# A hybrid Mamba/attention network on one core: the skip term D u on VectorE, and a PSUM bank of its own for each head's scores

## The chip, the cores and the metric

The kernel runs on one core of a Trainium2 chip. Five engines work from queues of their own, each in order: TensorE (PE; its weight loads are shown as PEld), VectorE (DVE), ScalarE (ACT), GpSimd (POOL) and SyncE (SP), which issues nearly all DMA transfers here. They meet through semaphores. Matmul results go to PSUM, which has eight banks of 512 fp32 columns in 128 partitions. The metric is the device time of one execution in microseconds.

## The reference

The input is x of (8, 384, 32, 32) in fp32: eight images (batches) of 1024 tokens with 384 channels. Two layers follow each other.

Layer 0 normalizes the tokens and runs a selective scan over them forward and, with the same weights, backward. For one direction (u is the convolved input after SiLU, z the gate, 16 states n per channel):

```python
def step(h, inp):
    dA, dBu, c = inp
    h = dA * h + dBu
    return (h, jnp.einsum('bdn,bn->bd', h, c))
...
y = ys.transpose(1, 0, 2) + u * D_param
y = y * silu(z)
return jnp.einsum('bld,od->blo', y, out_proj_w)
```

The two directions are added, scaled, joined with a local 3x3 convolution branch, and added to x.

Layer 1 is causal self-attention with 6 heads of 64, and then, on batches in 5 groups of one (`8 // 5`), a feed-forward network of width 1536 with sign-binarized weights and a quantization by the maximum of each group:

```python
scores = jnp.einsum('bhqd,bhkd->bhqk', q, k)
scores = jnp.where(causal, scores, -jnp.inf)
attn = jax.nn.softmax(scores, axis=-1)
out = jnp.einsum('bhqk,bhkd->bhqd', attn, v)
```

Batches past the fifth get attention only, since the groups don't reach them.

## The kernel before

Everything is fp32, with channels on the 128 partitions (3 chunks c of 384) and tokens along the free axis, in halves h of 512. A fp32 matmul shows as two MATMUL records.

**Stages.** For each batch there is `before_scan` (norm, input projections, convolutions, gates, delta), then the scan in units, then `attention`, and for five batches `feed_forward`. The program emits these as lists of small steps with rough costs. `spread_over` and the due times at the end of the function interleave them: scan units of later batches run beside attention, feed-forward and the `before_scan` of others. The last batch's attention stands alone at the end. The Tile framework then lays out each engine's queue by priorities and ready times of its own model, and gives tiles their buffers: a tile with a tag waits until one of the tag's `bufs` buffers is free.

**Scan.** A unit is one batch, one chunk c, one direction and half (`part`), and two states n: 768 units in all. `s_first` (L588) multiplies on GpSimd into a tile g (six buffers). `s_scan` makes exp(delta A) on ScalarE (L601), runs two scans on VectorE (L606) and one more GpSimd product (L612). `s_sum` (L620) adds the two states up over units: eight TensorE transposes of g into the PSUM bank y. After the last transposes g is free again. L636 and L641 take y to SBUF (yt).

**Gate.** `s_gate` runs 48 times, once for each batch, chunk and half. It loads halves of us (the sum of both directions' u) and of silu(z), each into a tile with one buffer (the DMA issues are recorded at L112, in `load`). In a bank of tag "pt" a matmul with the diagonal matrix diagd (L656) puts D u, and the transposes of the one or two yt tiles are added on it (L661). VectorE multiplies with the gate (L670), and SP stores the result (L672).

**Attention.** Heads go in pairs, two heads e to a chunk c: head e has partitions 64e to 64e+63 of q and k. `probabilities` calls `scores` 288 times in all: two matmuls (L788) into two PSUM tiles `ss`, one for each head, with e=1 first; the second, e=0, has a raised priority and is pinned behind what TensorE had before it in the program. Then, e=0 first, VectorE's tensor_tensor_reduce (L802, which shows as a custom instruction and a read of the accumulator) adds the mask, moves the tile out to SBUF and makes the row's extreme nm, and ScalarE takes the exponential (L812). `weighted_values` turns the probabilities over (L864, L866) and multiplies them with v (L877).

**PSUM banks.** `bank` hands out tiles of one bank each under five tags: y 1, da 2, s 2, pt 2, av 1, so all eight banks are taken. A call without a tag alternates between s and pt. Tag "s" serves the scores, the feed-forward matmuls (hp, yp, yq), and every other one of the projections (op, qp, vp, ap) and norms.

`pin` is the framework's `keep_in_program_order`: an instruction may not be queued ahead of the one that the program has before it on the same engine. It sets the order only, not a wait for its end, and others may come between.

Of the kernel before, what the change touches and what calls it, by code (L numbers as in the profile page):

```python
# [12 lines left out]
ALU = mybir.AluOpType  # L13
# [4 lines left out]
P = 128  # L18
B, C, H, W = 8, 384, 32, 32
L = H * W  # L20
NC = C // P
# [28 lines left out]
V_NORM, V_CW, V_CB, V_DTB, V_D, V_DW, V_DWB, V_BP, V_B2, V_ALOG = 0, 1, 5, 6, 7, 8, 17, 18, 19, 20  # L50
# [4 lines left out]
def kernel(  # L55
# [16 lines left out]
    nc = tc.nc  # L72
    pin = tc.keep_in_program_order
# [10 lines left out]
    def ctile(name, shape, dt=F32):  # L84
        return const.tile(shape, dt, name=name, tag=name)
# [4 lines left out]
    def mtile(name, n=L):  # L90
        return mid.tile([P, n], F32, name=name, tag="mid")
# [1 line left out]

    BANKS = {"y": 1, "da": 2, "s": 2, "pt": 2, "av": 1}
    turn = [0]

    def bank(name, tag=None):
        if tag is None:  # L100
            turn[0] += 1
            tag = ("s", "pt")[turn[0] % 2]
        return ps.tile([P, HB], F32, name=name, tag=tag, bufs=BANKS[tag])

    def half(h):
        return slice(h * HB, (h + 1) * HB)

    def chunk(c):
        return slice(c * P, (c + 1) * P)

    def load(dst, src):
        nc.sync.dma_start(out=dst, in_=src)  # L112
# [17 lines left out]
    vec = ctile("vec", [P, NC, NV])  # L130
# [8 lines left out]
    for d in range(2):  # L139
        nc.scalar.dma_start(out=wdt[d * DW : d * DW + RANK, :], in_=w_dt)  # L140
        nc.scalar.dma_start(
            out=wdt[d * DW + RANK : d * DW + RANK + 1, :],
# [13 lines left out]
    ident = ctile("ident", [P, P])  # L156
# [21 lines left out]
    amat = ctile("amat", [P, NC, NS])  # L178
    nc.scalar.activation(amat, vec[:, :, V_ALOG : V_ALOG + NS], AF.Exp)
    nc.vector.tensor_scalar(amat, amat, -1.0, None, ALU.mult)  # L180
    diagd = ctile("diagd", [P, NC, P])
    for c in range(NC):
        nc.vector.tensor_scalar(diagd[:, c, :], ident, vec[:, c, V_D : V_D + 1], None, ALU.mult)
    rssm = ctile("rssm", [P, 1])
    nc.vector.tensor_tensor(rssm, sc[:, 0:1], sc[:, 1:2], ALU.mult)
    rsh = ctile("rsh", [P, 1])
# [9 lines left out]
    def binarize(src, dst, nk, nout, per, name, emit):  # L196
# [15 lines left out]
        @emit  # L212
        def _():
            st["mps"] = bank(f"mps_{name}", "av")
# [44 lines left out]
    def mean_of(c_of, name):  # L259

        m = bank(name)
        for c in range(NC):
            nc.tensor.matmul(out=m, lhsT=onesc, rhs=c_of(c), start=(c == 0), stop=(c == NC - 1))  # L263
        return m
# [42 lines left out]
    def before_scan(b, tags, emit, later=None, diags=None):  # L307
# [5 lines left out]
        def bank_of(name):  # L313
            return bank(name, next(turns))
# [328 lines left out]
    def s_gate(u):  # L643

        if not u.last:
            return
        b, c, h = u.b, u.c, u.h
        yts = sst.pop(("yt", b, c, h))
        both = []
        for what in ("us", "z"):  # L650
            t = sp.tile([P, HB], F32, name=f"{what}h_{u.name}", tag=what, bufs=1)
            load(t, spilled[b, what, c][:, half(h)])
            both.append(t)
        us, sz = both
        tp = bank(f"yb_{u.name}", "pt")
        nc.tensor.matmul(  # L656
            out=tp, lhsT=diagd[:, c, :], rhs=us, start=True, stop=False, skip_group_check=True
        )
        for yt in yts:
            for i in range(QT):  # L660
                nc.tensor.matmul(  # L661
                    out=tp[:, chunk(i)],
                    lhsT=yt[:, i, :],
                    rhs=ident,
                    is_transpose=True,
                    start=False,
                    stop=(yt is yts[-1] and i == QT - 1),
                    skip_group_check=True,
                )
        nc.vector.tensor_tensor(sz, sz, tp, ALU.mult)  # L670
        t = dram.tile([P, HB], F32, name=f"sgy_{u.name}", tag=f"sp_gy_{c}_{h}")
        nc.sync.dma_start(out=t, in_=sz)  # L672
        spilled[b, "gy", c, h] = t


    def attention(b, emit_ffn, emit):
# [83 lines left out]
        def at_once(second):  # L760
            return tc.high_priority(offset=HURRY) if second else nullcontext()

        def rows_of(e):
            return slice(e * HD, (e + 1) * HD)

        def blocks_of(n):
            return [(k0, min(k0 + HB, n)) for k0 in range(0, n, HB)]

        def probabilities(c, g, steps):


            nb = g + 1

            def scores(i, qi, n, kb, k0, k1):
                pr = mtile(f"pr_{b}_{c}_{qi}_{kb}").rearrange("p (e l) -> p e l", e=2)
                st["pr", c, g, i, kb] = pr
                if kb == 0 and i == 0:
                    for what in ("nm", "rs"):
                        st[what, c, g] = small.tile(
                            [P, QT, 2, nb], F32, name=f"{what}_{b}_{c}_{g}", tag=f"{what}{nb}"  # L780
                        )
                nm, rs = st["nm", c, g], st["rs", c, g]
                ss = [bank(f"s_{b}_{c}_{qi}_{kb}_{e}", "s") for e in range(2)]

                order = (1, 0)
                for e in order:
                    with at_once(e == order[1]):
                        mm = nc.tensor.matmul(  # L788
                            out=ss[e][:, : k1 - k0],
                            lhsT=st["q"][rows_of(e), c, chunk(qi)],  # L790
                            rhs=st["k"][rows_of(e), c, k0:k1],
                            start=True,
                            stop=True,
                        )
                    if e == order[1]:
                        pin(mm)

                w = k1 - k0
                mask = cmask[:, HB - w :] if k1 == n else cmask[:, :1].to_broadcast([P, w])
                for e in range(2):  # L800
                    x, m = pr[:, e, :w], nm[:, i, e, kb : kb + 1]
                    nc.vector.tensor_tensor_reduce(  # L802
                        out=x,
                        in0=ss[e][:, :w],
                        in1=mask,
                        scale=-1.0,
                        scalar=-MASKED,
                        op0=ALU.add,
                        op1=ALU.min,
                        accum_out=m,  # L810
                    )
                    nc.scalar.activation(  # L812
                        x, x, AF.Exp, bias=m, scale=-1.0, accum_out=rs[:, i, e, kb : kb + 1]
                    )

            for i in range(QT):
                qi = g * QT + i
                n = (qi + 1) * P
                for kb, (k0, k1) in enumerate(blocks_of(n)):
                    steps(lambda i=i, qi=qi, n=n, kb=kb, k0=k0, k1=k1: scores(i, qi, n, kb, k0, k1))  # L820
# [275 lines left out]
    def slots(lo, hi):  # L1096
        def at(f, k):
            if 0 <= k < len(units):
                f(units[k])

        def slot(k):
            at(s_load, k + AHEAD + 2)
            at(lambda u: s_row(u, 0), k + AHEAD + 2)
            at(lambda u: s_row(u, 1), k + 2)
            at(s_first, k + AHEAD)
            at(s_scan, k)
            at(s_sum, k - 1)
            at(s_gate, k - 2)

        return [(lambda k=k: slot(k), 5.0) for k in range(lo, hi)]  # L1110
# [113 lines left out]
```

## Time and profile before

| what | value |
|---|---|
| median of 3 runs | 4989.93 us |
| lowest, highest | 4987.43, 4991.37 us |
| profiled execution | 4984.05 us |
| its span, first to last instruction | 4982.3 us |
| mean granted TensorE clock | 0.884 |
| scores, TensorE (L788) | 1152 records, 384.5 us occupied |
| scores, VectorE (L802) | 576 instructions, 299.5 us, 545 ns mean |
| gate, D u matmul (L656) | 96 records, 60.0 us occupied |
| gate, product (L670) | 48 instructions, 32.0 us |
| scans, VectorE (L606) | 1536 instructions, 1859.8 us |

Busy time is the time in which an engine had at least one instruction under way, so two matmuls side by side count once. A row of the profile's groups gives line, engine, operation, output and inputs, shapes and count, then the busy time with the mean of one instruction in ns, and after the second bar the idle time of the engine just before, with what ended it. A row of the waits gives engine and line, what was waited for, the sum in us, the number of times and the longest.

The attention stage runs from about 928 us for the first batch; the last batch's fills the end from about 4770 us on, with its scores from 4847 us.

### The profile page before, as it was taken

How to read it: one execution, taken by the hardware profiler on the slowest of the kernel's cores; microseconds unless marked ns; L12 is line 12 of the kernel's file. 1: busy time of each engine (PE TensorE's matmuls, PEld its weight loads, DVE VectorE, ACT ScalarE, POOL GpSimd, SP SyncE). 2: the span in 40 equal slices, each digit the busy share in tenths (PEclk: the TensorE clock that was granted, in tenths of full speed). 3: DMA queues.
4: the chain of work that ended last, by engine and by line, in shares of the span. 5: the costliest groups of instructions: out<-in, count | busy, mean ns of one | idle time of the engine just before them, and what ended most of it. 6: DMA issues, size and time to landing. Idle time of an engine off the chain costs nothing. (4 is left out here: it accounts for less than half of the span.)

```text
span 4982.3 us, 50788 instructions
## 1 busy us (share of the span) xinstructions
PE 4058.8 (81%) x16458; PEld 2192.3 (44%) x16458; DVE 3607.8 (72%) x4771; ACT 2668.1 (54%) x4858; POOL 3696.0 (74%) x1944
## 2 busy tenths in 40 slices
PE   3687786988888888788787888887888988888989
PEld 1243343544444444345443444443454544444444
DVE  6887988677886768786778867687867676676623
ACT  4575655565554655545656446555456365464425
POOL 0578687997768986779876788867789888888800
PEclk7788797899989899888998888998899988999999
DMA  6554646324463335463334633334533333334210
GB/s 230 204 185 151 200 164 229 114 93 130 140 220 120 112 116 168 136 200 123 100 125 147 210 111 129 112 130 157 193 130 116 113 110 124 131 102 137 93 58 26
DMA packets 365010, 696.36 MB, mean 140 GB/s; under 512 B 30104, under 2 KB 88904, under 8 KB 364744
## 3 DMA queue, kind: packets, MB, share of 16 engines
q1 hardware_dynamic: 355232, 676.97, 40.9%
q10 hardware_dynamic: 9512, 16.15, 0.9%
q8 instruction: 130, 2.13, 0.2%
q14 instruction: 136, 1.11, 0.1%
HBM read 527.33 MB, written 165.68 MB: 139 GB/s over the span
## 5 line engine op out<-in xcount | busy, mean ns | idle before, releaser
L588 POOL TENSOR_TENSOR g<-ud,bc 128x1024 f32<-128x1024 f32 x768 | 1840.4, 2396 | 579.8 <-PE y L620 452.0
L612 POOL TENSOR_TENSOR g<-g,bc 128x1024 f32<-128x1024 f32 x768 | 1822.1, 2373 | 251.7 <-DVE g L606 157.8
L601 ACT ACTIVATE da<-dl,amat 128x512 f32<-128x512 f32 x1536 | 1057.3, 691 | 1532.5 <-DVE g L606 1498.3
L606 DVE TENSOR_TENSOR_SCAN g<-da,g 128x512 f32<-128x512 f32 x768 | 906.5, 1210 | 475.4 <-POOL g L588 457.2
L606 DVE TENSOR_TENSOR_SCAN g<-da,carry,g 128x512 f32<-128x512 f32 x768 | 953.3, 1271 | 384.2 <-POOL g L588 354.1
L620 PE MATMUL y<-ident,g 128*128 128x128 f32 x6144 | 949.1, 303 | 266.7 <-POOL g L612 123.1
L620 PEld LDWEIGHTS y<-ident,g 128*128 128x128 f32 x6144 | 789.3, 156 | 714.4 <-issue 418.9
L788 PE MATMUL s<-k,q 64*128 64x512 f32 (+3 forms) x1152 | 384.5, 600 | 128.9 <-DVE nm L802 110.5
L802 DVE CUSTOM_DVE_ANT_0 pr<-s,cmask 128x512 f32<-128x512 f32 (+3 forms) x576 | 299.5, 545 | 178.2 <-PE s L788 177.9
L812 ACT ACTIVATE pr<-pr,nm 128x512 f32<-128x512 f32 (+3 forms) x576 | 348.9, 607 | 123.5 <-DVE nm L802 121.6
L864 PE MATMUL pt<-ident,pr 128*128 128x128 f32 x1728 | 304.0, 309 | 93.6 <-ACT ptn L866 55.1
L995 PE MATMUL hp<-t,w 128*128 128x512 f32 x720 | 334.9, 610 | 28.7 <-DMA w<-w1s 18.3
L1039 PE MATMUL yp<-h,w 128*128 128x512 f32 x720 | 332.6, 620 | 15.3 <-DMA w<-w2s 12.1
L864 PEld LDWEIGHTS pt<-ident,pr 128*128 128x128 f32 x1728 | 217.7, 155 | 245.0 <-ACT ptn L866 110.3
L877 PE MATMUL av<-ptn,v 128*64 128x512 f32 (+3 forms) x1152 | 273.1, 555 | 50.4 <-ACT ptn L866 33.9
L341 PE MATMUL in<-xn,win 128*128 128x512 f32 x576 | 282.3, 636 | 32.3 <-DVE xc L463 8.6
L866 ACT COPY ptn<-pt 128x512 f32<-128x512 f32 (+3 forms) x576 | 255.3, 472 | 49.8 <-PE pt L864 48.4
L727 PE MATMUL qp<-t,wqk 128*128 128x512 f32 x576 | 266.4, 613 | 11.7 <-DVE t L302 9.1
L400 DVE SCALAR_TENSOR_TENSOR loc<-xn,vec,loc 128x496 f32<-128x496 f32 (+3 forms) x384 | 259.9, 721 | 19.5 <-ACT loc L389 18.2
L788 PEld LDWEIGHTS s<-k,q 64*128 64x128 f32 x1152 | 132.3, 206 | 261.2 <-DVE nm L802 179.6
L611 POOL COPY carry<-g 128x2 f32<-128x2 f32 x384 | 87.0, 226 | 205.9 <-DVE g L606 205.8
L1039 PEld LDWEIGHTS yp<-h,w 128*128 128x128 f32 x720 | 142.0, 201 | 189.1 <-issue 169.4
(153 smaller groups left out, 4722.4 us busy)
## 6 DMA issues: line engine op xcount, KB each, us to landing
bc<-rows SPq DMA_DIRECT2D x512, 512.0 KB, 4.1
dl<-sdl SPq DMA_DIRECT2D x160, 256.0 KB, 2.9
ud<-sud SPq DMA_DIRECT2D x160, 256.0 KB, 2.7
t<-st SPq DMA_DIRECT2D x63, 512.0 KB, 5.1
su<-u SPq DMA_DIRECT2D x48, 512.0 KB, 3.4
du<-su SPq DMA_DIRECT2D x96, 256.0 KB, 3.8
sdl<-du SPq DMA_DIRECT2D x96, 256.0 KB, 2.8
sud<-du SPq DMA_DIRECT2D x96, 256.0 KB, 2.3
```

Source lines behind the costliest of these rows:

```text
L341: nc.tensor.matmul(out=mp, lhsT=st["win", c][:, k, i, :], rhs=st["xn"][:, k, half(h)], start=(k == 0), stop=(k == NC - 1),)
L588: pin(nc.gpsimd.tensor_tensor(g, ud, sst["bc", 0, u.b, u.part, u.n], ALU.mult))
L601: nc.scalar.activation(da, sst["dl", u.b, u.c, u.part], AF.Exp, scale=amat[:, u.c, n : n + 1])
L606: nc.vector.tensor_tensor_scan(gi[:, ::step], da[:, ::step], gi[:, ::step], first, ALU.mult, ALU.add)
L612: pin(nc.gpsimd.tensor_tensor(g, g, sst["bc", 1, u.b, u.part, u.n], ALU.mult))
L620: nc.tensor.matmul(out=y[:, j, :], lhsT=g[:, i, chunk(j)], rhs=ident, is_transpose=True, start=(u.opens and i == 0 and j == 0), stop=(u.cl ...
L788: mm = nc.tensor.matmul(out=ss[e][:, : k1 - k0], lhsT=st["q"][rows_of(e), c, chunk(qi)], rhs=st["k"][rows_of(e), c, k0:k1], start=True, st ...
L802: nc.vector.tensor_tensor_reduce(out=x, in0=ss[e][:, :w], in1=mask, scale=-1.0, scalar=-MASKED, op0=ALU.add, op1=ALU.min, accum_out=m,)
L812: nc.scalar.activation(x, x, AF.Exp, bias=m, scale=-1.0, accum_out=rs[:, i, e, kb : kb + 1])
L864: nc.tensor.transpose(pt[:, chunk(i)], pr[:, e, chunk(j % QT)], ident)
L995: nc.tensor.matmul(out=hp, lhsT=st["w1"][:, c, chunk(m % 2)], rhs=st["xn"][:, c, half(h)], start=(c == 0), stop=(c == NC - 1),)
L1039: nc.tensor.matmul(out=yp, lhsT=st["w2", k // 6][:, k % 6, :], rhs=st["h", k // NC][:, k % NC, half(h)], start=(k == 0), stop=(k == NF - 1),)
```

## The change

Two edits that don't depend on each other.

In the gate the matmul with diagd is gone, and with it diagd itself. The first transpose now starts the bank, and after the last one VectorE adds us times D to the bank, in PSUM, ahead of the product with silu(z).

The tag "s" with two buffers becomes two tags with one buffer each, s0 and s1. Callers that ask for "s" get them in turn, by a counter of their own, in program order. `scores` asks for s0 for e=0 and for s1 for e=1. The VectorE instruction that empties the bank of e=1 (`order[0]`, the head whose matmul goes first) is pinned behind the one of e=0.

```diff
-    BANKS = {"y": 1, "da": 2, "s": 2, "pt": 2, "av": 1}
-    turn = [0]
+    BANKS = {"y": 1, "da": 2, "s0": 1, "s1": 1, "pt": 2, "av": 1}
+    turn = [0, 0]
...
             tag = ("s", "pt")[turn[0] % 2]
+        if tag == "s":
+            turn[1] += 1
+            tag = ("s0", "s1")[turn[1] % 2]
         return ps.tile([P, HB], F32, name=name, tag=tag, bufs=BANKS[tag])
...
-    diagd = ctile("diagd", [P, NC, P])
-    for c in range(NC):
-        nc.vector.tensor_scalar(diagd[:, c, :], ident, vec[:, c, V_D : V_D + 1], None, ALU.mult)
...
         tp = bank(f"yb_{u.name}", "pt")
-        nc.tensor.matmul(
-            out=tp, lhsT=diagd[:, c, :], rhs=us, start=True, stop=False, skip_group_check=True
-        )
         for yt in yts:
             for i in range(QT):
                 nc.tensor.matmul(
...
-                    start=False,
+                    start=(yt is yts[0] and i == 0),
                     stop=(yt is yts[-1] and i == QT - 1),
                     skip_group_check=True,
                 )
+        nc.vector.scalar_tensor_tensor(tp, us, vec[:, c, V_D : V_D + 1], tp, ALU.mult, ALU.add)
         nc.vector.tensor_tensor(sz, sz, tp, ALU.mult)
...
-                ss = [bank(f"s_{b}_{c}_{qi}_{kb}_{e}", "s") for e in range(2)]
+                ss = [bank(f"s_{b}_{c}_{qi}_{kb}_{e}", f"s{e}") for e in range(2)]
...
-                    nc.vector.tensor_tensor_reduce(
+                    moved = nc.vector.tensor_tensor_reduce(
...
+
+                    if e == order[0]:
+                        pin(moved)
```

## The prediction

> **What bounds the kernel now.** I read the page from the top. Its first part gives the engines' shares, its second shows that no engine is full for the whole run:
>
> ```profile
> PE 4058.8 (81%) x16458; PEld 2192.3 (44%) x16458; DVE 3607.8 (72%) x4771; ACT 2668.1 (54%) x4858; POOL 3696.0 (74%) x1944
> ...
> PE   3687786988888888788787888887888988888989
> DVE  6887988677886768786778867687867676676623
> POOL 0578687997768986779876788867789888888800
> PEclk7788797899989899888998888998899988999999
> ```
>
> TensorE is the busiest engine, at 8 to 9 tenths nearly everywhere. GpSimd, which makes two passes over every scan unit, fills 7 to 9 tenths between slice 2 and slice 38. VectorE passes 8 tenths only in some slices. PEclk says that TensorE ran at 0.7 to 0.9 of its clock, and the page's mean is 0.884.
>
> Next I asked who waits for whom, and for the stages with scores the busy time by window:
>
> ```profile
> POOL g L588 <- PE y L620: 452.0, 202, 14.1
> PE s L788 <- DVE nm L802: 110.5, 89, 3.4
> SPq L112 <- PE yb L656: 201.5, 34, 22.4
> SPq L112 <- DMA sgy<-zh: 51.0, 32, 4.7
> ...
> 928.00:1150.00 222.00, 178.77 (x1005) 103.41 (x1004) 162.79 (x270) 141.21 (x325) 205.79 (x109) 0.91 0.30 98
> 2270.00:2470.00 200.00, 157.85 (x881) 91.89 (x881) 146.35 (x254) 123.26 (x287) 181.45 (x94) 0.89 0.37 119
> 4840.00:4982.00 142.00, 132.37 (x705) 64.62 (x703) 53.67 (x183) 82.50 (x232) 0.00 (x0) 0.98 0.06 23
> ```
>
> The columns of the windows are the stretch, its length, and the busy time of PE, PEld, DVE, ACT and POOL. In the two attention stages shown POOL is 93% and 91% busy, PE 81% and 79%. Over all seven attention stages beside scans (1662 us) POOL is busy for 1473 us, so 189 us are idle, and 174 us of that is POOL waiting for the transposes of L620, which free its buffers g and stand late in TensorE's queue. So TensorE paces POOL there through its order. In the last stage (from 4840 us) there is no scan left and PE is 93% busy: work taken off it there comes off the end directly.
>
> **The scores' matmuls.** The groups by form show what the change aims at, beside the gate's rows:
>
> ```profile
> L788 PE MATMUL s<-k,q 64*128 64x512 f32 x576 | 221.5, 716 | 39.7 <-DVE nm L802 39.4
> L877 PE MATMUL av<-ptn,v 128*64 128x512 f32 x576 | 165.9, 656 | 16.5 <-DVE o L891 16.5
> L656 PE MATMUL yb<-ush,diagd 128*128 128x512 f32 x96 | 60.0, 712 | 3.7 <-ACT ptn L866 1.8 <-DVE du L527 1.1 <-ACT u L379 0.5
> L369 DVE SCALAR_TENSOR_TENSOR u<-up,vec,u 128x512 f32<-128x512 f32 x90 | 66.0, 745 | 3.4 <-ACT u L358 3.3
> ...
> 2283.70 2.07 PE L788 MATMUL s<-k,q 64*128 64x512 f32 x2
> 2285.70 0.90 PE L620 MATMUL y<-ident,g 128*128 128x128 f32 x3
> 2286.53 2.07 PE L788 MATMUL s<-k,q 64*128 64x512 f32 x2
> ...
> 2289.36 2.10 PE L788 MATMUL s<-k,q 64*128 64x512 f32 x4
> ```
>
> One fp32 matmul is two records. A pair of heads uses the array's upper and lower 64 rows. At 2289.36 all four records of a pair took 2.10 us side by side (at a low clock); at 2283.70 and 2286.53 each head's two records took 2.07 us alone, 4.14 us for the pair. In the last stage a full-clock pair takes 1.13 us side by side. L877 has the same columns and counts, all side by side: 165.9 us of occupancy against 221.5.
>
> **What the Trainium skill says.** "TensorE: Matmul & The Clock Gate", section "The mechanism" (of packing small matmuls): matmuls in different row groups run together, so a pack costs about one matmul. The trace agrees (2.10 us against 2 x 2.07). "TensorEngine Tiling (Array Packing)", section "Gotcha 1: PSUM Pressure": row tiles write to different banks and may not share one at a time. So a pair needs both banks free, and the 110.5 us above are that wait. The same first page, section "What's actually happening": a TensorE that was idle runs at half clock until it has been busy for a while. The doubled durations at 2283 us fit; so relief of TensorE may come back in part as a lower clock.
>
> **The change part by part, against the profiled execution** (4984.05 us, span 4982.3; the median of the runs shown is 5.9 us above it).
>
> 1. *Own banks and the tied order.* Before, the head that goes first (e=1) takes whichever of two banks is free, and the other waits for VectorE: half-array runs. After, e=1 needs s1, whose reader is tied behind that of s0, so both are free when e=1 starts, and e=0 follows at once. Occupancy: L788 now takes 221.5+77.7+49.6+36.0 = 384.8 us over its four widths, L877 165.9+47.5+36.1+23.6 = 273.1. In the last stage a paired L788 takes 0.05 us more than a paired L877 (1.13 to 1.08, 0.92 to 0.87), so 273.1 + 288 x 0.05 = 287.5 us is to be had: 97 us less. Not all of it is time: the first matmul ran in a gap that now is waiting, unless something else is queued there. Following the 288 pairs through the trace, 148 aren't in step (or ran at a low clock); if each starts only when both banks are empty and nothing fills the wait, they end some 37 us earlier in sum. Bounds 37 and 97; I take 60, since the order of TensorE's queue is laid out with the wait known, and other ready work (L620, L864) can go ahead.
>
> 2. *D u leaves TensorE.* 96 records, 60.0 us (1.25 us per gate, 48 gates), go. Their weight loads lie beside other work. diagd's three instructions at 15 us (0.8 us) go too and VectorE has 12 us of waiting for DMA there: 0.
>
> 3. *D u comes to VectorE.* 48 scalar_tensor_tensor of 128x512, one operand and the result in PSUM. Nearest row L369, same kind: 66.0/90 = 0.73 us each, 35 us in sum. "VectorE: DVE Perf Modes", "The perf-mode tier table", gives fp32 with a PSUM operand one element per cycle, which agrees. Behind it on VectorE stand the gate's L670 and then scans. The gate itself gets shorter: 1.25 + 1.16 (eight transposes, 55.5/48) + 0.67 before, 1.16 + 0.73 + 0.67 after, so the pt bank isn't held longer and the 27.0 and 22.5 us of L864 for zh don't grow.
>
> 4. *The single buffer of us* is freed by VectorE's new instruction in place of TensorE's first: later by 1.16 us and up to one pair of scans (2.5 us). SP's next load of us stands waiting for that (201.5 us now). But the load of z right behind it waits for the store of zh anyway, which comes later still. Cost 0; if other loads stood between, POOL's waits for bc (32 us in all) would grow.
>
> 5. *The other users of s* (hp, yp, yq, qp, op, ap, vp) now alternate between s0 and s1 by the program's order rather than taking a free one. Each has a short life and they already alternate: 0, bounds -5 and +15.
>
> Sum. TensorE is relieved by 60 + 60 = 120 us. How much of that reaches the end: 1 in the last stage, and elsewhere what POOL's wait for L620 gives back; I take one half (bounds 0.2 and 0.9): -60. VectorE's 35 us are mostly covered by its waits for POOL g L588 (811 us); I take three tenths (0.1 to 0.7): +11. Together -49, so 4935 for the profiled execution and **4941** as a median. The likeliest case's own range: best 157 x 0.9 - 4 = 137 less (4853), worst 97 x 0.2 - 25 = 6 more; most of it lies in 4885 to 4985.
>
> **Rivals.**
>
> *No change, 4990.* POOL sets the pace (93% busy in the first attention stage), the pairs that were in step already (140 of 288) gain nothing, and what TensorE saves turns into idling or a lower clock. For: POOL's share. Against: its 452 us of waiting for TensorE. The case that the change doesn't do what it says falls here too: the order on VectorE is tied, but if scans stand between the two readers the pair only waits longer.
>
> *Slower, 5040: the tie turns overlap into a stall of TensorE's in-order queue.* Between the two readers of one pair VectorE ran one scan in 47 and two in 38 of the 288 pairs, 1.2 us each. Then the head of TensorE's queue waits for the second reader, with L620 behind it and POOL behind L620. Before, one half pair ran in that gap. Price: about 1.8 us for each such pair. It decides once the added idling passes 157 us: with the 110.5 us that are waited now, at (157+110)/1.8, about 150 pairs. At 200 pairs TensorE loses 360 - 110 - 157 = 93 us; a half of it and 11 us for VectorE is +58, 5048 us; with fewer pairs, and VectorE's whole 35 us on the path, about 5025. I put the case at 5040. For: the planned order can move scans into the gap on purpose. Against: where the halves run one after the other, a pair that starts after both banks are free still ends no later.
>
> **How the numbers follow.** A change of under 0.2% (10 us) can't be told from none here. Likeliest case 0.56 at 4941, no change 0.12, the stall 0.24, and 0.08 for a general reordering of the four queues to the worse (the planner sees other ready times everywhere; 5000 to 5030). Faster takes most of the first and a little of the second; slower takes the last two and a rest: 0.56, 0.10, 0.34. The range 4885 to 5035 leaves out the tails of the first case and of the stall.
>
> **What will show it.** Right: L656 gone, L788's occupancy near 290 us with 64x512 near 175, the new VectorE row at 48 x 0.73 us, POOL's wait for L620 well below 452 us. Wrong: PE's wait for nm L802 rising from 110.5 to over 250 us (the stall), or POOL's wait for L620 unchanged with PE's share lower (no change), or PEclk below 0.86 (relief lost to the clock). I would be most wrong if the order of the queues changes far from the scores and the gates.

## The result: no change that counts

Medians of twenty runs of each: 4993.4 us after the change (4979.62 to 5006.32) and 4988.61 us before (4963.89 to 4998.86). The ratio is 1.0013 with an interval of 1.0003 to 1.0024. The ratio lies inside the 0.2% that were called no change; the interval reaches a little past it and leaves out 1, so after is at most a trifle slower. The forecast was 4941 us. The profiled execution of after has a span of 4996.3 us.

The first two parts of the page of after, to be laid beside the same lines of before:

```profile
PE 3961.8 (79%) x16362; PEld 2136.7 (43%) x16362; DVE 3624.4 (73%) x4821; ACT 2656.1 (53%) x4849; POOL 3703.2 (74%) x1944
...
PE   4687786877788788788787887888877878878888
PEclk7787797899989899888898898998898989989999
```

TensorE is occupied for 97 us less (4058.8 to 3961.8), at the same mean clock (0.884 before, 0.885 after), and the kernel is no faster. The groups of after by form, and then its waits (engine and line, what was waited for, us in total, times, longest), say where both edits show:

```profile
L786 PE MATMUL s<-k,q 64*128 64x512 f32 x576 | 191.8, 747 | 108.3 <-DVE nm L800 107.6
L667 DVE SCALAR_TENSOR_TENSOR yb<-ush,vec,yb 128x512 f32<-128x512 f32 x48 | 35.8, 745 | 30.9 <-PE yb L658 25.2 <-issue 2.9 <-ACT da L601 2.7
```

```profile
POOL g L588 <- PE y L620: 447.9, 174, 15.0
PE s L786 <- DVE nm L800: 155.0, 97, 5.8
PE pt L865 <- ACT ptn L867: 97.8, 73, 4.6
SPq L115 <- DVE yb L667: 224.4, 25, 50.8
```

Two waits of before that go beside these and beside later ones:

```profile
DVE g L606 <- POOL g L588: 811.3, 448, 10.2
PE pt L864 <- ACT ptn L866: 55.1, 43, 3.8
```

The change does what it says. The 512-wide scores take 191.8 us of TensorE in place of 221.5 (all four widths 311 in place of 385), and VectorE has its 48 new instructions. But TensorE now waits 155.0 us for emptied score banks (110.5 before) and 97.8 us for the copies ptn (55.1 before). GpSimd's wait for the transposes of y, which I had named as the gauge of a gain, stands where it was: 447.9 us against 452.0.

### The profile page after: what moved, and what is told of

The parts are those of the page before. It is cut to its first block, busy times and chain, and to the rows that moved or that the text cites. A ratio compares the mean times of both kernels' runs of the same rounds, so it can differ in the third digit from the quotient of the medians.

```text
span 4996.3 us, 50656 instructions
## 1 busy us (share of the span) xinstructions
PE 3961.8 (79%) x16362; PEld 2136.7 (43%) x16362; DVE 3624.4 (73%) x4821; ACT 2656.1 (53%) x4849; POOL 3703.2 (74%) x1944
## 5 line engine op out<-in xcount | busy, mean ns | idle before, releaser
L588 POOL TENSOR_TENSOR g<-ud,bc 128x1024 f32<-128x1024 f32 x768 | 1847.4, 2406 | 579.4 <-PE y L620 447.9
L620 PE MATMUL y<-ident,g 128*128 128x128 f32 x6144 | 955.3, 302 | 258.8 <-POOL g L612 127.9
L620 PEld LDWEIGHTS y<-ident,g 128*128 128x128 f32 x6144 | 790.5, 156 | 666.4 <-issue 400.8
L786 PE MATMUL s<-k,q 64*128 64x512 f32 (+3 forms) x1152 | 311.4, 621 | 176.8 <-DVE nm L800 155.0
L865 PE MATMUL pt<-ident,pr 128*128 128x128 f32 x1728 | 319.9, 305 | 139.2 <-ACT ptn L867 97.8
L996 PE MATMUL hp<-t,w 128*128 128x512 f32 x720 | 336.6, 613 | 39.3 <-DMA w<-w1s 30.5
L996 PEld LDWEIGHTS hp<-t,w 128*128 128x128 f32 x720 | 134.9, 196 | 194.4 <-issue 152.4
```

What stands on the lines that cost most here:

```text
L588: pin(nc.gpsimd.tensor_tensor(g, ud, sst["bc", 0, u.b, u.part, u.n], ALU.mult))
L620: nc.tensor.matmul(out=y[:, j, :], lhsT=g[:, i, chunk(j)], rhs=ident, is_transpose=True, start=(u.opens and i == 0 and j == 0), stop=(u.cl ...
L786: mm = nc.tensor.matmul(out=ss[e][:, : k1 - k0], lhsT=st["q"][rows_of(e), c, chunk(qi)], rhs=st["k"][rows_of(e), c, k0:k1], start=True, st ...
L865: nc.tensor.transpose(pt[:, chunk(i)], pr[:, e, chunk(j % QT)], ident)
L996: nc.tensor.matmul(out=hp, lhsT=st["w1"][:, c, chunk(m % 2)], rhs=st["xn"][:, c, half(h)], start=(c == 0), stop=(c == NC - 1),)
```

## The experiments

All ratios below are against the kernel before on the same chip, with a 95% interval. Beside the ratio one length is used throughout. The score stages are the seven stretches from the first scores' matmul of a batch to its last `ap` matmul that lie beside scans; their sum is read from each trace by the starts of those instructions, one profiled execution of each kernel. "Rest" is the span less that sum, the last batch's attention in it.

### Each edit alone

`gate_only` has the gate's part of the diff shown above and nothing else; `banks_tie` has the banks and the tie. In `no_du` the term D u is left out:

```diff
-        nc.tensor.matmul(
-            out=tp, lhsT=diagd[:, c, :], rhs=us, start=True, stop=False, skip_group_check=True
-        )
...
-                    start=False,
+                    start=(yt is yts[0] and i == 0),
```

Expected of the gate alone:

> The kernel before with the gate's edit alone: D u off TensorE (60.0 us occupied), on VectorE (35.8 us). Theory 1 (GpSimd's products and the in-order loop around them pace the scan, so 1% of work more or less on TensorE or VectorE isn't seen): within 0.2% of before, 4979 to 4999 us. Theory 2 (the two edits have effects of opposite sign that cancel): this one is off by over 0.4%, faster if TensorE's relief is worth something (under 4970), slower if VectorE is the dear engine (over 5010).

Of the banks with the tie:

> The kernel before with the other edit alone: own banks and the tied order. Theory 1: within 0.2% of before; TensorE's occupancy by the scores falls from 385 to about 311 us and its waiting for the emptied banks rises from 110 to about 155 us. Theory 2: off by over 0.4% with the sign opposite to that of the gate's edit.

Of the kernel without D u:

> The kernel before without the term D u (the matmul is left out, nothing takes its place), so 60 us less on TensorE and nothing more on VectorE. Theory 1: within 0.2% of before, as POOL is no faster. Theory 2, or TensorE as the bound: 30 us faster or more, under 4960.

Measured: `gate_only` 4948.65 us, ratio 0.9929 (0.9910 to 0.9947). `no_du` 4955.15 us, 0.9939 (0.9925 to 0.9953). `banks_tie` 5032.44 us, 1.0096 (1.0080 to 1.0112). Theory 1 falls three times. Two effects of opposite sign cancel: 0.9929 x 1.0096 = 1.0024 for a measured 1.0013. The waits of GpSimd for y (the transposes of L620) follow the time. In `gate_only` and then in `banks_tie`, where the lines are numbered differently (L617 and L623 are the transposes of y):

```profile
POOL g L585 <- PE y L617: 399.6, 185, 14.9
```

```profile
POOL g L591 <- PE y L623: 489.7, 190, 14.1
PE s L791 <- DVE nm L805: 162.8, 99, 5.8
DVE g L609 <- POOL g L591: 896.7, 497, 9.3
```

452 us before, 52 less with the gate's edit, 38 more with the banks and the tie. The stage sums say where:

```
kernel       span   score stages   rest
before       4982       1692       3290
gate_only    4963       1670       3293
no_du        4953       1669       3284
banks_tie    5027       1734       3293
after        4996       1700       3296
```

The gains and losses lie in the score stages (-22, -23, +42 us); what lies outside them moves by 6 us or less. The profiled execution of `gate_only` is the slowest of its six (4964.74 us), so its -22 may be too small.

### Is it TensorE's work, or a changed order?

`pe_twice` issues the gate's matmul of before twice into the same bank, so TensorE has 96 more records of that kind and no other instruction is added:

```diff
         nc.tensor.matmul(
             out=tp, lhsT=diagd[:, c, :], rhs=us, start=True, stop=False, skip_group_check=True
         )
+        nc.tensor.matmul(
+            out=tp, lhsT=diagd[:, c, :], rhs=us, start=True, stop=False, skip_group_check=True
+        )
```

> The kernel before with the D u matmul issued twice into the same bank (the second overwrites the first), 60 us more on TensorE and nothing else. If TensorE's time is worth one half at the gate, as the version without D u says (31 us for 60): 0.4 to 0.8% slower, 5006 to 5026 us. If that gain was of the planned order and not of the work: within 0.3%.

Measured: 5025.72 us, 1.0064 (1.0047 to 1.0080), so +32 us for one D u matmul more in each gate (0.64% of 4991), beside -30 us for one less in `no_du` (0.61% of 4986). The score stages take 1723 us, 31 more than before. The two rows of D u in `pe_twice`:

```profile
L656 PE MATMUL yb<-ush,diagd 128*128 128x512 f32 x96 | 60.1, 712 | 9.1 <-DVE du L525 3.8 <-DMA ush<-sus 2.3 <-ACT ptn L869 1.4
L659 PE MATMUL yb<-ush,diagd 128*128 128x512 f32 x96 | 55.6, 664 | 0.0
```

So the matmul at the gate is worth about one half of its 60 us, in both directions, which speaks against the gain of `no_du` being an accident of the planned order. Why one half is open, and the traces allow two readings. First, the 60 us are not all spent on D u alone: for 14 of them, in before, another matmul is under way as well, and TensorE's busy time as a whole falls by 32 us in `no_du` (4058.8 to 4026.6) and rises by 41 in `pe_twice` (to 4100.1). Second, 24 of the 48 gates, with 30.5 of the 60.0 us, lie inside the score stages, which is where the time changes: the work may count nearly whole there and little elsewhere.

`gate_more` has the gate's edit with VectorE's new instruction issued twice:

```diff
+        nc.vector.scalar_tensor_tensor(tp, us, vec[:, c, V_D : V_D + 1], tp, ALU.mult, ALU.add)
         nc.vector.scalar_tensor_tensor(tp, us, vec[:, c, V_D : V_D + 1], tp, ALU.mult, ALU.add)
```

> The gate's edit alone, with VectorE's new instruction issued twice in each gate (D u is added twice), so 36 us more on VectorE, 72 us in all against none in the kernel before. If VectorE's work here is covered by its waiting for GpSimd: within 0.3% of the version with it once (0.9929), 0.990 to 0.996 against before. If three tenths of it is on the path, as predicted: 11 us more, 0.995. If VectorE is what paces the gates' stages: 1.000 or more.

Measured: 4946.2 us, 0.9929 (0.9909 to 0.9950), the same as with it once. Its groups:

```profile
L664 DVE SCALAR_TENSOR_TENSOR yb<-ush,vec,yb 128x512 f32<-128x512 f32 x48 | 35.7, 744 | 37.3 <-PE yb L655 26.4 <-issue 6.1 <-ACT da L598 2.8
L665 DVE SCALAR_TENSOR_TENSOR yb<-ush,vec,yb 128x512 f32<-128x512 f32 x48 | 35.4, 738 | 0.1
```

and one of its waits:

```profile
DVE g L603 <- POOL g L585: 720.1, 421, 8.6
```

71 us of VectorE's time cost nothing measurable. `no_du` has neither the matmul nor VectorE's instruction and stands at 0.9939; three tenths of 71 us would have put `gate_more` 21 us behind it, at 0.998, which lies outside its interval. In `gate_only` the same wait is longer:

```profile
DVE g L603 <- POOL g L585: 742.8, 434, 9.8
```

So the second instruction's 35 us shorten VectorE's waiting for GpSimd by 23 us.

### What the banks cost, and what the tie

`banks_free` is `banks_tie` without the two lines of the tie; `tie_shared` is the tie on the two shared banks of before:

```diff
-                    moved = nc.vector.tensor_tensor_reduce(
+                    nc.vector.tensor_tensor_reduce(
...
-                    if e == order[0]:
-                        pin(moved)
```

> Own banks, but the order of the two emptying instructions not tied. Theory 1: within 0.3% of before. The tie as the cost (rival of the prediction): clearly faster than the version with the tie, by 0.5% or more, with the wait of TensorE for the banks back near 110 us. If the tie does nothing the planned order is the same, and so is the time.

> The tie alone, on the two shared banks of before. Theory A: the first matmul takes the bank that is emptied first, so the overlap stays: within 0.4% of before. Theory B: the cost is that of the tie, 0.7 to 1.1% slower.

Measured: `banks_free` 4988.11 us, 1.0008 (0.9993 to 1.0022); `tie_shared` 5051.61 us, 1.0117 (1.0098 to 1.0136). The banks of their own change nothing by themselves: without the tie the scores still take 390.7 us of TensorE. The tie in this order (e=0, then e=1) is the loss, whatever the banks. My explanation of that moment (theory A, the first matmul needs the bank that is emptied last) had `tie_shared` within 0.4%, and fell.

Two kernels turn the order round. `tie_back` empties e=1 first, as the matmuls go, and ties e=0 behind it. `paired_alt` is the same, but the heads change banks from call to call, so that the first matmul again needs the bank that is emptied last:

```diff
-                for e in range(2):
+                for e in order:
...
-                    if e == order[0]:
+                    if e == order[1]:
                         pin(moved)
```

```diff
-                ss = [bank(f"s_{b}_{c}_{qi}_{kb}_{e}", f"s{e}") for e in range(2)]
+                flip[0] += 1
+                ss = [
+                    bank(f"s_{b}_{c}_{qi}_{kb}_{e}", f"s{(e + flip[0]) % 2}") for e in range(2)
+                ]
```

> Own banks and a tied order, but the other way round: VectorE empties e=1's bank first, then e=0's, the order in which the matmuls go. Theory A (the tie costs because the first matmul then needs the bank that is emptied last, so TensorE and VectorE no longer overlap on one pair): e=1's matmul can start while e=0's bank is still being emptied, so the cost is gone: within 0.3% of before, occupancy of the scores back near 385 us. Theory B (any fixed order lets VectorE put scans ahead of the pair): still 0.6% slower or more. Theory C (side by side is what is wanted, the loss has another cause): no better than the version with the tie, 1.0096.

> As the version that is tied the other way round (e=1 emptied first), but the banks change sides from call to call, so that e=1's matmul needs the bank that was emptied last and the pair goes side by side again. Theory A1 (what costs is that a pair waits for both banks, so that no half is computed while the other half's bank is being emptied): 0.6 to 1.1% slower than before, occupancy of the scores near 311 us, TensorE's wait for the banks above 150 us. Theory A2 (what costs is that VectorE may not begin with e=1): within 0.3% of before.

Measured: `tie_back` 4979.97 us, 0.9979 (0.9968 to 0.9990), with the scores at 386.5 us; `paired_alt` 4993.54 us, 1.0006 (0.9994 to 1.0017). A fixed order as such (theory B) isn't the cost, then, and neither is the waiting for both banks (theory A1). The row of the scores in the groups of `paired_alt`, and three of its waits:

```profile
L795 PE MATMUL s<-k,q 64*128 64x512 f32 (+3 forms) x1152 | 306.8, 607 | 175.3 <-DVE nm L809 158.5 <-ACT v L756 11.0 <-DVE v L756 5.4
```

```profile
DVE g L610 <- POOL g L592: 808.3, 456, 7.9
POOL g L592 <- PE y L624: 475.5, 199, 14.1
PE s L795 <- DVE nm L809: 158.5, 108, 5.3
```

This separates the two halves of the edit. Pairs side by side (306.8 us in place of 384.5) are worth nothing: of the 78 us saved, 48 come back at once as TensorE's waiting for the banks (158.5 to 110.5), and the time does not move. The loss goes with the order e=0, then e=1: the two kernels with that tie and the gate of before lose about 1%, whether the pairs go in step (`banks_tie`) or not (`tie_shared`, with the scores at 389.4 us), and the two that are tied the other way don't. The exponentials on ScalarE stand in the same loop and were turned round with the emptyings; the two were not tried apart.

The 0.2% of `tie_back` should not be read as a gain. VectorE's instructions come in nearly the same sequence there as in `banks_free` (the same operation, tiles and shape in 4697 of 4773 places, where `banks_tie` agrees with `banks_free` in 3517), and `banks_free` stands at 1.0008. This says something of before, too: without a tie the planner seems to empty e=1 first already. The trace doesn't name the heads, but in 36 pairs of before, and in 33 of `banks_free`, the first emptying begins before the last record of the pair's matmuls, which is e=0's, has started, so it must be that of e=1. In `banks_tie`, `tie_shared` and after there is no such pair.

What does that order change? Two stretches of the timelines show it (start, us, engine, line, operation, and in brackets the idle time before and what ended it). First `paired_alt`, e=1 first; L795 is the pair's matmuls, L610 a scan, and L809 empties a bank:

```profile
2311.01 0.70 PE L795 MATMUL s<-k,q 64*128 64x256 f32 x4 [1.83 <-DVE nm L809]
2315.62 1.13 PE L795 MATMUL s<-k,q 64*128 64x512 f32 x4 [2.41 <-DVE nm L809]
...
2312.01 0.40 DVE L809 CUSTOM_DVE_ANT_0 pr<-s,cmask 128x256 f32<-128x256 f32 x1
2312.33 0.08 DVE L809 DVE_READ_ACCUMULATOR2_ANT nm<- 128x1 f32 x1
2314.01 1.22 DVE L610 TENSOR_TENSOR_SCAN g<-da,g 128x512 f32<-128x512 f32 x1 [1.60 <-POOL g L592]
2315.16 0.40 DVE L809 CUSTOM_DVE_ANT_0 pr<-s,cmask 128x256 f32<-128x256 f32 x1
2315.48 0.08 DVE L809 DVE_READ_ACCUMULATOR2_ANT nm<- 128x1 f32 x1
2315.48 1.22 DVE L610 TENSOR_TENSOR_SCAN g<-da,g 128x512 f32<-128x512 f32 x1
```

Then `banks_tie`, e=0 first, where L609 is the scan and L805 empties, with the matmuls of the same pair and of the next one first:

```profile
2320.44 0.70 PE L791 MATMUL s<-k,q 64*128 64x256 f32 x4
2324.59 1.82 PE L791 MATMUL s<-k,q 64*128 64x512 f32 x4 [1.65 <-DVE nm L805]
...
2321.53 2.34 DVE L609 TENSOR_TENSOR_SCAN g<-da,g 128x512 f32<-128x512 f32 x2 [1.70 <-POOL g L591]
2323.78 0.40 DVE L805 CUSTOM_DVE_ANT_0 pr<-s,cmask 128x256 f32<-128x256 f32 x1
2324.11 0.08 DVE L805 DVE_READ_ACCUMULATOR2_ANT nm<- 128x1 f32 x1
2324.11 0.42 DVE L805 CUSTOM_DVE_ANT_0 pr<-s,cmask 128x256 f32<-128x256 f32 x1
```

In `banks_tie` the pair's matmuls are over at 2321.1 us. VectorE's queue has both scans of a unit next, which take 2.34 us and don't start before 2321.53, since they wait for GpSimd; both emptyings stand behind them. In `paired_alt` the first emptying of the same pair comes at 2312.01, 0.3 us after its matmuls, and the second between the two scans. Over the 252 pairs beside scans, read from the starts and ends in the traces (a scan counts in the gap if any part of it lies there):

```
kernel       pair's end to start    scans in    pairs with a scan        ratio
             of first emptying      that gap    between the emptyings
before            0.77 us             0.83            92                 1
tie_back          0.80                0.84            92                 0.9979
paired_alt        1.24                1.01            63                 1.0006
tie_shared        1.78                1.32             0                 1.0117
banks_tie         2.05                1.48             0                 1.0096
```

In step or not, the kernels in which the two emptyings stand together, mostly behind scans, lose 1%. That the planner puts them there because it takes e=0's matmul for finished later than e=1's is a guess from the order; it was not tested by itself.

How the late emptying turns into lost time isn't shown either. It is not TensorE's wait for these banks: that is about as long in `paired_alt` (158.5 us) as in `banks_tie` (162.8), and in the stretches above the next pair comes no sooner in `paired_alt`. What differs is VectorE's wait for GpSimd in the scans, 808.3 against 896.7 us, and GpSimd's for the transposes of y, 475.5 against 489.7. The queues differ in many other places as well, so a part of the 1% may lie in what the planner moved elsewhere.

`tie_hurry` is `banks_tie` with the emptying instructions at a raised priority:

```diff
-                    moved = nc.vector.tensor_tensor_reduce(
+                    with tc.high_priority(offset=HURRY):
+                        moved = nc.vector.tensor_tensor_reduce(
...
```

> Own banks, the tie, and a raised priority for the two emptying instructions, so that no scan that is ready later goes ahead of them. Theory B: the 0.9% comes back, within 0.3% of before, and TensorE's wait for the banks falls from 163 us to 110 or less. Theory A: at most half of it comes back, 0.4% slower or more.

Measured: 5024.64 us, 1.0068 (1.0046 to 1.0091). Some 0.3 points less are lost than in `banks_tie`, but the two intervals overlap; the wait of TensorE for the banks doesn't fall (171.2 us), and the gap to the first emptying stays at 2.06 us. A higher priority doesn't undo the order; so theory B, in the form that a priority mends it, isn't borne out, and whether any of the loss came back stays open.

### Versions that were meant to be faster

`gate_back` joins the gate's edit with the banks of `tie_back`. `gate_back_y` adds a raised priority for the transposes in `s_sum`:

```diff
-                nc.tensor.matmul(
-                    out=y[:, j, :],
+                with tc.high_priority(offset=60):
+                    nc.tensor.matmul(
+                        out=y[:, j, :],
...
```

> The gate's edit and own banks, with VectorE emptying e=1 first. If the two effects add: 0.9929 x 0.9979 = 0.991, about 4945 us, 0.7% or more faster than before.

> The version just above, with the transposes that free GpSimd's buffers (in s_sum) at a raised priority in TensorE's queue. If GpSimd's wait for them (450 us) is what makes TensorE's work dear, that wait falls and the time goes below 4930 us; if the transposes only push the attention's matmuls back, within 0.3% of the version above.

Measured: `gate_back` 4944.83 us, 0.9915 (0.9898 to 0.9932), as expected; its interval overlaps that of `gate_only` (0.9910 to 0.9947), so these two can't be told apart, and that `tie_back`'s 0.2% adds to the gate's gain isn't shown. Both are faster than before and after. `gate_back_y` took 5026.71 us, 1.0079 (1.0066 to 1.0093): GpSimd's wait for y went up, not down, from 389.1 us in `gate_back` to 477.2 us. Its score stages take 1668 us against 1644, and its rest 3356 against 3282, so it loses inside and outside of them. Moving the transposes ahead in the queue by this priority doesn't shorten that wait.

## Why the prediction was wrong

Its pieces, against what the runs showed:

1. *Own banks and the tied order: this step failed.* It counted the tie as free and the freed TensorE time as 60 us of useful relief, "since the order of TensorE's queue is laid out with the wait known, and other ready work (L620, L864) can go ahead". The occupancy did fall, by 73 us rather than 97. But side-by-side pairs are worth 0 (`paired_alt`, 1.0006): 48 of the 78 us return as waiting for banks. And the tie, put at nothing, costs 0.9 to 1.2% (`banks_tie` 1.0096, `tie_shared` 1.0117), since it takes the emptying of e=1 back behind that of e=0 and both behind VectorE's scans. The wait for banks, 110.5 us before, grew to 155.0. The term was -30 us in the sum and measures +48 (0.96% of 4986).
2. *D u leaves TensorE: right in size.* 60 us at one half is -30; `no_du` gives -30, `pe_twice` +32. The half was a guess between 0.2 and 0.9, and what sets it is open.
3. *D u comes to VectorE: too dear.* Predicted +11 of 35 us; `gate_more` shows no cost for 71 us (0.9929, beside 0.9939 without any in `no_du`).
4. *The single buffer of us: right as far as seen.* SP's wait for it rose from 201.5 to 224.4 us, and `gate_only`, which has it too, is faster.
5. *The other users of s: right.* `banks_free` 1.0008, with an interval that holds 1.

The measured time is near that of the rival "no change, 4990", but not for its reason: the pace of GpSimd did not hide the two effects, they cancelled. That their sizes matched is luck.

The rival "slower, 5040" named the engines of the loss, VectorE's scans ahead of its emptying, and came near the size, for `banks_tie` stands at 5032. It had the scans in the wrong spot. It looked for them between the two readers of a pair and made the case depend on their number there; the tie takes them out from between and puts both readers together behind them. The count was off as well: the trace of before has one scan between the readers in 92 pairs and two in none, in place of one in 47 and two in 38. And its mark, a wait of TensorE for the banks of over 250 us, was not met (155.0 after, 162.8 in `banks_tie`). It was also set against the gate's gain as if only one of the two could win.

The general mechanism, that GpSimd's wait for L620 passes TensorE's delays on, fits most runs: 389 to 406 us in the four kernels at 0.99 (`gate_only`, `no_du`, `gate_more`, `gate_back`), 448 to 476 in those at about 1, 486 to 496 in `pe_twice`, `banks_tie`, `tie_shared` and `tie_hurry`. This is a wait that goes along with the time, not a proof that it makes it; `gate_back_y`, the one run that aimed at it, has 477.2 us at 1.0079.

A small misreading of the page: GpSimd's digits fall to 5 and 6 in some slices between the second and the thirty-eighth, not only to 7.

## What to carry to other kernels

Occupancy saved on an engine is not yet time saved: here 60 us of TensorE were worth 30 at the gate, and 78 were worth nothing at the scores, where 48 of them came back as waiting. When an order is tied on an engine, look in the trace for the order that the planner had chosen before, and for what goes ahead of the tied pair afterwards. And run two unrelated edits apart, since a null result can be a gain and a loss of the same size.

## What had not been expected

VectorE, at 72% of the span, took 71 us more at the gates without any change in time (0.9929 both with 36 and with 71 us), while a matmul of 60 us on TensorE, at 81%, moved it by 0.6% either way. The busy shares of the two engines differ by 9 points only.
